# A decoder layer on one core: the column sums of the context's codes move from the matrix engine to accumulating transfers

## The chip, the cores and the metric

The kernel runs on 1 core of one Trainium2 chip. The metric is the device time of one execution in microseconds (us), less is better. The core has a matrix engine (TensorE, "PE" in the profile, with "PEld" for its weight loads), VectorE ("DVE"), ScalarE ("ACT"), GpSimd ("POOL") and a queue of its own for transfers (SyncE, "SP"). Each engine works through its instructions in one order that is fixed when the kernel is built; an instruction that waits holds those behind it on its engine.

## The reference

One decoder layer over `x` (2 x 512 tokens, 1024 wide), cut to what matters:

```python
x = layernorm(x + attention(x))                     # per token, over 32 x 32 head dimensions
# cross step: both operands are rounded to 256 codes, then one product per batch element
def fake_quant(x, s, z):
    q = clip(round(x / s + z), 0, 255)
    return (q - z) * s
x = layernorm(x + fake_quant(x, s1, z1) @ fake_quant(ctx, s2, z2))   # ctx: 2 x 1024 x 1024
...
h = relu(x @ up_w) ** 2
shared = h @ down_w                                  # 1024 -> 2048 -> 1024
moe = ((x @ fc1_w) @ expert_w) * (sum of the two largest of x @ gate_w)
x = layernorm(x + layernorm(shared + moe @ fc2_w) * gamma + beta)
```

The kernel keeps codes, not the dequantised values: `cq` holds 255 minus the code of the context, in two bytes, and `a` holds the code of `x` less 128. Expanding the product of (code - zero point) leaves three terms: the product of the codes, a term per token (`r`), and a term per column that holds the sum of a context's codes over its 1024 rows. That last term is the row `crow`.

## The kernel before, in words

Tokens are worked in 8 tiles of 128 (`t` = 0 to 7), two tiles to a block, four blocks; tiles 0 to 3 belong to context 0, tiles 4 to 7 to context 1. A context is 8 tiles of 128 rows (`KC` = 8), all kept in `cq`.

*The front.* `fill` (L398) projects tiles 2 to 7 to q, k and v, writes them to scratch with accumulating transfers (L195, L196), brings them back later (L179, L180), and makes `e2`, a product of two weights (L458). Beside it `context_tiles` (L537) loads context 0 on SyncE's queue and turns each tile into codes with three ScalarE steps (L375, L378, L381), from 32.6 to 71.5 us.

*The token path* (`token_path`, L683) runs, tile by tile, the scores and attention on VectorE (L474 to L518), a layernorm, then `cross`. Layernorms that run aside (`normalise_aside`) take ScalarE's square and variance (L351, L353), one power on GpSimd (`rstd`, L355), and ScalarE's shift and scaling (L359, L360). `cross` (L616) makes the codes `a` on ScalarE (the last step L644; tile 1 is "hurried" and uses VectorE, L364 to L366), turns them with TensorE (`pta`, L652; L630 for tile 1), copies them out (`aT`), adds `r` and `crow` to the tokens on VectorE (L658, L659), multiplies codes with codes (`py`, L665, two halves of 8 products), and adds the result (L670). The tokens are then turned (`pt_x`, L134) for the feed-forward part.

*The row.* `context_row` (L584) makes `crow` before `cross` of the first tile of a context: two halves, for each a bank `pc` of PSUM, eight products of a matrix of ones with the eight tiles of codes (L591), and one ScalarE step (L594).

*The feed-forward part* of blocks 0 and 1 (`ffn`, products `pu` and `pl` at L827, `pd` at L1057) runs on TensorE beside the token path of the following blocks; blocks 2 and 3 are done together at the end (L942, L1317). `context_beside` (L549) makes the codes of context 1 beside block 0: it loads on GpSimd's queue (L558), does two steps for three tiles early, waits until tile 3's `py` is done (`cq` has one buffer), and writes the rest (L577) from 254.0 to 283.5 us.

*What sets the order.* Instructions are ordered on each engine when the kernel is built, by the order in which the generators above are advanced (the numbers they yield are weights), and by `issue_after`, which lays an instruction behind another one of the same engine. `behind_products` lays the token path's products behind the last feed-forward product laid so far; the `e2` products of the second half are laid behind `codes_turned`, the transposes of tile 1's codes. `spare_bank` (L605) gives a bank of `ps_dn` in the front and while a block's `up` products run, else one of `ps_mm`.

Of the kernel before, what the change touches and what calls it, by code (L numbers as in the profile page):

```python
# [8 lines left out]

F32 = mybir.dt.float32  # L10
BF16 = mybir.dt.bfloat16
AF = mybir.ActivationFunctionType
ALU = mybir.AluOpType
AX = mybir.AxisListType
# [2 lines left out]
P = 128  # L17
# [10 lines left out]
def kernel(  # L28
# [24 lines left out]
    nc = tc.nc  # L53

    B, S, E = x.shape
# [9 lines left out]
    KC = NCTX // P  # L65
# [6 lines left out]
    HALF = 512  # L72
# [30 lines left out]

    ident = const.tile([P, P], F32, name="ident")
    make_identity(nc, ident)
    identb = const.tile([P, P], BF16, name="identb")
    nc.vector.tensor_copy(identb, ident)
    onesb = const.tile([P, P], BF16, name="onesb")
    nc.vector.memset(onesb, 1.0)
    neg_half = const.tile([P, 1], F32, name="neg_half")  # L110
    nc.vector.memset(neg_half, -0.5)

# [115 lines left out]
    def keep_awake(n):  # L228

        ps = ps_mm.tile([P, HALF], F32, tag="mm", name="awake")  # L230
        for _ in range(n):
            laid[0] = nc.tensor.matmul(
                ps.rearrange("p (a b) -> p a b", b=P), onesb,
                onesb.unsqueeze(1).to_broadcast([P, HALF // P, P]), start=True, stop=True,
            )

    qkv = {}
# [100 lines left out]
    def normalise_aside(t, sums, name):  # L338

        n = sums.shape[-1]  # L340
        parts = small.tile([P, 2], F32, tag="parts", name=f"parts_{name}")
        minus = parts[:, 0:1]
        if n > 1:
            minus = small.tile([P, 1], F32, tag="minus", name=f"minus_{name}")
        with behind_acted(True):
            nc.scalar.activation(
                parts[:, 0:n], sums, AF.Copy, scale=-1.0 / E, accum_out=minus if n > 1 else None
            )
        square = attp.tile([P, E], BF16, tag="square", name=f"square_{name}")
        total = small.tile([P, 1], F32, tag="square", name=f"squares_{name}")  # L350
        nc.scalar.activation(square, t, AF.Square, bias=minus, accum_out=total)  # L351
        ve = small.tile([P, 1], F32, tag="ve", name=f"ve_{name}")
        nc.scalar.activation(ve, total, AF.Identity, scale=1.0 / E, bias=eps)  # L353
        rstd = small.tile([P, 1], F32, tag="rstd", name=f"rstd_{name}")
        nc.gpsimd.tensor_tensor(rstd, ve, neg_half, ALU.pow)  # L355
# [176 lines left out]

    made = []

    def context_tiles(b):  # L537

        cq = cqs[b] = tokp.tile([P, KC, E], BF16, tag="cq", name=f"cq_{b}")
        for k in range(KC):  # L540
            stage = work.tile([P, E], F32, tag="work", name=f"ctx_{b}_{k}")
            nc.sync.dma_start(stage, ctx_in[b, ts(k, P), :])
            with tc.issue_after(turned[0].ins):
                for _ in below_top(cq[:, k, :], stage, stage, rs2, z2):
                    pass
            made.append((b, k))
            yield

    def context_beside(b):  # L549
# [17 lines left out]
                yield  # L567
        while b * (S // P) - 1 not in crossed:
            yield
        cq = cqs[b] = tokp.tile([P, KC, E], BF16, tag="cq", name=f"cq_{b}")  # L570
        for k in range(KC):
            if k not in passes:
                passes[k] = below_top(None, stages[k], stages[k], rs2, z2)
            for _ in passes[k]:
                yield
            with behind_acted(True):
                nc.scalar.activation(  # L577
                    cq[:, k, :], stages[k], AF.Relu, scale=-1.0, bias=top_down
                )
            made.append((b, k))  # L580
            load(k + 3)
            yield

    def context_row(b, cq):  # L584
        crow = tokp.tile([P, E], F32, tag="crow", name=f"crow_{b}")
        for h in range(E // HALF):
            pc = spare_bank(f"pc_{b}_{h}")

            with tc.issue_after(projecting[0].ins) if b == 0 else behind_products():
                for k in range(KC):  # L590
                    nc.tensor.matmul(  # L591
                        pc, onesb, cq[:, k, ts(h, HALF)], start=(k == 0), stop=(k == KC - 1)
                    )
# [19 lines left out]

        return tc.issue_after(lately[0].ins) if lately[0] is not None else ExitStack()

    def cross(t, xc, cq, crow, between):  # L616


        hurried = t == TB - 1
        tmp = work.tile([P, E], F32, tag="work", name=f"qt_{t}")  # L620
        a = attp.tile([P, E], BF16, tag="a", name=f"a_{t}")
        aT = tokp.tile([P, KC, P], BF16, tag="aT", name=f"aT_{t}")
        if hurried:

            quantise(a, xc, tmp, rs1, z1)
            yield 2.2
            pt = ps_tr.tile([P, KC, P], BF16, tag="tr", name=f"pta_{t}")
            with behind_products():
                for k in range(KC):
                    codes_turned[0] = nc.tensor.transpose(pt[:, k, :], a[:, ts(k, P)], identb)  # L630
            nc.scalar.copy(aT, pt)
            yield 1.0
            total = ps_tr.tile([P, 2], F32, tag="tr", name=f"pr_{t}")
            with tc.issue_after(expert[0].ins):
                for k in range(KC):
                    nc.tensor.matmul(
                        total, aT[:, k, :], onesb[:, 0:2], start=(k == 0), stop=(k == KC - 1)
                    )
            total = total[:, 0:1]
        else:  # L640
# [5 lines left out]
            )  # L646
            yield 2.0
            yield from between
            pt = ps_tr.tile([P, KC, P], BF16, tag="tr", name=f"pta_{t}")
            with behind_products():  # L650
                for k in range(KC):
                    nc.tensor.transpose(pt[:, k, :], a[:, ts(k, P)], identb)  # L652
            nc.scalar.copy(aT, pt)  # L653
            yield 4.0
        behind = ExitStack if hurried or t == NT - 1 else lambda: tc.issue_after(lowered[0].ins)
        r = small.tile([P, 1], F32, tag="r", name=f"r_{t}")
        with behind():
# [25 lines left out]
    def token_path():  # L683
# [25 lines left out]
        for blk in range(NBLK):  # L709
            xcs = []  # L710
            x2T = []
            for i in range(TB):
# [9 lines left out]
                if t % (S // P) == 0:  # L722
                    b = t // (S // P)
                    while len(made) < (b + 1) * KC:
                        yield 1.0
                    batch = cqs[b], context_row(b, cqs[b])
                between = scores_left(t + 1) if t + 1 < NT else ()
                last = yield from cross(t, xc, *batch, between)

                def hand_over(blk=blk, t=t, i=i, xc=xc, x2T=x2T):  # L730
                    if not x2T:
# [416 lines left out]
    def down_pair(outer):  # L1148
# [118 lines left out]
        def end_aside(i):  # L1267
# [8 lines left out]
            square = attp.tile([P, E], BF16, tag="square", name=f"summed_{i}")  # L1276
# [210 lines left out]
```

## Time and profile before

| | us |
|---|---|
| median of 3 runs (704.29 to 704.39) | 704.35 |
| the profiled execution, its time | 704.49 |
| its span, first to last instruction | 702.7 |
| TensorE busy / VectorE / ScalarE / GpSimd | 682.4 / 586.5 / 261.8 / 77.0 |
| moved by DMA | 139.08 MB, 198 GB/s over the span |
| mean granted TensorE clock | 0.991 |

How to read the views shown later. In an order of time, a row has its start, its length, the engine, the line of the kernel, the operation, the tile written and those read, the sizes and the count, and in brackets the idle time before it and what ended that. In a tile's answer, three lengths in ns are the least, the median and the largest. A DMA row ends with the median time from issue to landing. Products are pipelined, so the length of one is not what it costs TensorE.

### The profile page before, as it was taken

The page shows a single profiled execution, that of the slowest core. Times are in us where ns is not written, and L with a number is a line of the kernel's source. Part 1 is how long each engine was busy: PE and PEld are TensorE (multiplying, and loading weights), DVE is VectorE, ACT ScalarE, POOL GpSimd, SP SyncE. Part 2 cuts the span into 40 slices and gives each one's busy share as a digit, 9 for nine tenths or more (in the row PEclk, how much of TensorE's full clock was granted, in tenths as well). Part 3 has the DMA queues.
Part 4 walks back from the last instruction along what each step waited for, and adds up shares of the span by engine and source line. Part 5 has one row for each costly group of instructions (what it writes and reads, how often), then busy time and mean ns, then how long its engine had stood idle before and what let it go on. Part 6 is the DMA issues. An engine that isn't in the chain of part 4 may idle for free.

```text
span 702.7 us, 7462 instructions
## 1 busy us (share of the span) xinstructions
PE 682.4 (97%) x2812; PEld 482.6 (69%) x2812; DVE 586.5 (83%) x678; ACT 261.8 (37%) x440; POOL 77.0 (11%) x107
## 2 busy tenths in 40 slices
PE   8999999999999999999999999999999999999991
PEld 4666654578876444478876444488888888888881
DVE  5899987699999999799999950397787688897895
ACT  1287544222635458426736132212251200000252
POOL 1012112100011122001002000020010000001012
PEclk9999999999999999999999999999999999999996
DMA  9999528485446458446436534667897445556733
GB/s 336 304 346 370 127 32 290 116 288 175 135 132 174 178 194 254 134 166 215 145 119 177 182 120 126 238 194 242 338 344 254 164 166 171 168 197 192 207 84 120
DMA packets 70900, 139.08 MB, mean 198 GB/s; under 512 B 5264, under 2 KB 39696, under 8 KB 70864
## 3 DMA queue, kind: packets, MB, share of 16 engines
q1 hardware_dynamic: 60656, 106.87, 44.9%
q0 software_dynamic: 10064, 31.47, 16.3%
q8 instruction: 22, 0.36, 0.2%
q10 hardware_dynamic: 144, 0.26, 0.1%
q14 instruction: 14, 0.11, 0.0%
HBM read 114.99 MB, written 21.50 MB: 194 GB/s over the span
## 4 chain that ended last, share of the span: by engine, by line
PE 44%; issue 5%; ACT 3%; DVE 2%; POOL 1%; POOLq 0%
PE pd L1057 9%; PE pp L942 9%; PE ps L1317 7%; PE pp_mm L942 5%; PE pp_tr L942 4%; PE ps_mm L1317 4%; PE ps_tr L1317 3%; PE pu L827 2%; ACT square L351 1%; PE py L665 1%; POOL rstd L355 1%; DVE pav L507 1%; PE pl L827 1%; PE pt_x L134 0%; ACT xc L360 0%
## 5 line engine op out<-in xcount | busy, mean ns | idle before, releaser
L1057 PE MATMUL pd<-dn,h 128*128 128x512 f32 x320 | 139.3, 593 | 0.0
L827 PE MATMUL pu<-x2T,up 128*128 128x256 f32 x512 | 113.1, 380 | 0.8 <-ACT relu L843 0.8
L1057 PEld LDWEIGHTS pd<-dn,h 128*128 128x128 f32 x320 | 60.3, 190 | 71.8 <-issue 71.3
L827 PEld LDWEIGHTS pu<-x2T,up 128*128 128x128 f32 x512 | 96.4, 190 | 15.0 <-ACT relu L843 1.2
L507 DVE TENSOR_TENSOR pav<-s,v 128x2048 f32<-128x2048 f32 x32 | 72.5, 2282 | 0.0
L474 DVE TENSOR_TENSOR pqk<-qk 128x2048 f32<-128x2048 f32 x32 | 72.5, 2283 | 0.0
L480 DVE TENSOR_REDUCE s<-pqk 128x256 f32<-128x2048 f32 x32 | 72.3, 2278 | 0.1
L513 DVE TENSOR_REDUCE o<-pav 128x64 f32<-128x2048 f32 x32 | 72.0, 2266 | 0.0
L157 PE MATMUL pqk<-wqkv,xT 128*128 128x512 f32 x128 | 63.4, 595 | 1.2 <-DVE wqkv L249 0.9
L162 PEld LDWEIGHTS pv<-wqkv,xT 128*128 128x128 f32 x128 | 24.3, 190 | 24.2 <-issue 22.5
L355 POOL TENSOR_TENSOR rstd<-ve,neg_half 128x1 f32<-128x1 f32 x21 | 21.6, 1028 | 174.7 <-ACT ve L353 171.4
L162 PE MATMUL pv<-wqkv,xT 128*128 128x256 f32 x128 | 35.6, 379 | 0.0
L670 DVE SCALAR_TENSOR_TENSOR xc<-py,ns,xc 128x512 f32<-128x512 f32 x16 | 11.7, 743 | 26.4 <-PE py L665 26.4
L157 PEld LDWEIGHTS pqk<-wqkv,xT 128*128 128x128 f32 x128 | 23.6, 190 | 11.4 <-issue 4.3
L843 ACT ACTIVATE relu<-pu 128x256 f32<-128x256 f32 x32 | 12.1, 377 | 51.5 <-PE pu L827 51.5
L665 PE MATMUL py<-cq,aT 128*128 128x512 bf16 x128 | 28.9, 379 | 0.9 <-ACT aT L653 0.9
L1221 DVE TENSOR_TENSOR tt<-dn 128x1024 f32<-128x1024 f32 (+1 forms) x20 | 21.2, 1060 | 10.2 <-DMA dn<-in_L_ffn_down_w_dram 5.8
L458 PE MATMUL pe<-fc,exT 128*128 128x512 f32 x64 | 28.7, 594 | 0.0
L827 PE MATMUL pl<-x2T,fc 128*128 128x256 f32 x128 | 28.2, 380 | 0.5 <-ACT latent L856 0.5
L827 PEld LDWEIGHTS pl<-x2T,fc 128*128 128x128 f32 x128 | 24.2, 190 | 4.3 <-ACT latent L856 0.9
L665 PEld LDWEIGHTS <-aT 128*128 128x128 bf16 x128 | 12.4, 98 | 17.0 <-issue 2.0
L653 ACT COPY aT<-pta 128x1024 bf16<-128x1024 bf16 x7 | 7.0, 1007 | 43.9 <-PE pta L652 43.9
(311 smaller groups left out, 1165.5 us busy)
## 6 DMA issues: line engine op xcount, KB each, us to landing
up<-in_L_ffn_up_w_dram SPq DMA_DIRECT2D x16, 1024.0 KB, 5.5
dn<-in_L_ffn_down_w_dram SPq DMA_DIRECT2D x16, 1024.0 KB, 5.0
pair<-in_L_ffn_up_w_dram SPq DMA_DIRECT2D x8, 1024.0 KB, 6.3
dn<-tw SPq DMA_DIRECT2D x8, 1024.0 KB, 5.1
tw<-outer POOLq DMA_DIRECT2D x7, 1024.0 KB, 5.1
fc<-in_L_ffn_fc_w_dram SPq DMA_DIRECT2D x6, 1024.0 KB, 5.6
dn<-in_L_ffn_down_w_dram SPq DMA_DIRECT2D x12, 512.0 KB, 5.6
outer<-in_L_ffn_down_w_dram SPq DMA_DIRECT2D x5, 1024.0 KB, 5.1
```

The source lines that it names most:

```text
L157: projecting[0] = nc.tensor.matmul(pqk, xT[:, k, :], wqkv[k][:, 0 : 2 * DG], start=(k == 0), stop=(k == KE - 1))
L162: nc.tensor.matmul(pv[:, :DG], xT[:, k, :], wqkv[k][:, 2 * DG : 3 * DG], start=(k == 0), stop=(k == KE - 1),)
L458: expert[0] = nc.tensor.matmul(ps, exT[m // 2][:, m % 2, ts(l, P)], fc2[m // 2][:, m % 2, ts(n, HALF)], start=(m == 0), stop=(m == NL - 1),)
L474: nc.vector.tensor_tensor(prod.rearrange("p (d e g) -> p d e g", d=DC, g=G), q3[:, ts(c, DC), :].unsqueeze(2).to_broadcast([P, DC, D, G]), ...
L480: nc.vector.tensor_reduce(s[:, ts(c, DC), :].rearrange("p d e -> p (d e)"), prod.rearrange("p (c g) -> p c g", g=G), AX.X, ALU.add,)
L507: nc.vector.tensor_tensor(prod.rearrange("p (d g e) -> p d g e", d=DC, g=G), s[:, ts(c, DC), :].unsqueeze(2).to_broadcast([P, DC, G, D]), ...
L513: nc.vector.tensor_reduce(o[:, ts(c, DC), :].rearrange("p d g -> p (d g)"), prod.rearrange("p (c e) -> p c e", e=D), AX.X, ALU.add,)
L665: crossed[t] = nc.tensor.matmul(py, aT[:, k, :], cq[:, k, ts(h, HALF)], start=(k == 0), stop=(k == KC - 1))
L827: lately[0] = nc.tensor.matmul(ps[:, :NB], ws[:, k, wcols], xT[:, k, :], start=(k == 0), stop=(k == KE - 1))
L942: lately[0] = nc.tensor.matmul(banks[m], steps[g][m][:, k, :], moving[m][:, k, :], start=(k == 0 and m not in (6, 3, 7)), stop=(k == KH - ...
L1057: lately[0] = nc.tensor.matmul(pd[i][n], h[:, kk // 4, i, kk % 4, :], w[:, k, ts(n, HALF)], start=(kk == 0), stop=(kk == NK - 1),)
L1317: lately[0] = nc.tensor.matmul(banks[mm], unit(o, mm, j), inner_weights[o, cc][mm][:, j - lo, :], start=(j == 0 and mm not in FIRST_OF), s ...
```

## The change

After each tile of codes is made, a transfer on GpSimd's queue takes it into one more tile in SBUF, `codes_b` (128 x 1024): the first copies, the seven that follow add. Each of the eight accesses the same tile, so each waits for the one before. A sum of eight codes is at most 2040, which a 16-bit float of eleven significant bits holds exactly; `bfloat16` has eight, so all two-byte tiles of the kernel become `float16`. `context_row` then needs one product with the ones for each half instead of eight, and is called later: inside `cross`, after the codes of the context's first token tile are turned, just before `r`, `crow` and `py`.

```diff
-BF16 = mybir.dt.bfloat16
+F16 = mybir.dt.float16
...
-    identb = const.tile([P, P], BF16, name="identb")
+    identh = const.tile([P, P], F16, name="identh")
-    onesb = const.tile([P, P], BF16, name="onesb")
+    onesh = const.tile([P, P], F16, name="onesh")
...
-    made = []
+    made, code_sums = [], {}
+
+    def add_codes(b, k):
+
+        if k == 0:
+            code_sums[b] = tokp.tile([P, E], F16, tag="codes", name=f"codes_{b}")
+            nc.gpsimd.dma_start(code_sums[b], cqs[b][:, k, :])
+        else:
+            nc.gpsimd.dma_start(code_sums[b], cqs[b][:, k, :], accum_op=ALU.add)
 
     def context_tiles(b):
 
-        cq = cqs[b] = tokp.tile([P, KC, E], BF16, tag="cq", name=f"cq_{b}")
+        cq = cqs[b] = tokp.tile([P, KC, E], F16, tag="cq", name=f"cq_{b}")
         for k in range(KC):
             stage = work.tile([P, E], F32, tag="work", name=f"ctx_{b}_{k}")
             nc.sync.dma_start(stage, ctx_in[b, ts(k, P), :])
             with tc.issue_after(turned[0].ins):
                 for _ in below_top(cq[:, k, :], stage, stage, rs2, z2):
                     pass
+            add_codes(b, k)
             made.append((b, k))
             yield
...
                 nc.scalar.activation(
                     cq[:, k, :], stages[k], AF.Relu, scale=-1.0, bias=top_down
                 )
+            add_codes(b, k)
             made.append((b, k))
             load(k + 3)
             yield
 
-    def context_row(b, cq):
+    crows = {}
+
+    def context_row(b):
         crow = tokp.tile([P, E], F32, tag="crow", name=f"crow_{b}")
         for h in range(E // HALF):
             pc = spare_bank(f"pc_{b}_{h}")
 
             with tc.issue_after(projecting[0].ins) if b == 0 else behind_products():
-                for k in range(KC):
-                    nc.tensor.matmul(
-                        pc, onesb, cq[:, k, ts(h, HALF)], start=(k == 0), stop=(k == KC - 1)
-                    )
+                nc.tensor.matmul(
+                    pc, onesh, code_sums[b][:, ts(h, HALF)], start=True, stop=True
+                )
...
-    def cross(t, xc, cq, crow, between):
+    def cross(t, xc, b, between):
 
 
         hurried = t == TB - 1
+        cq = cqs[b]
...
             nc.scalar.copy(aT, pt)
             yield 4.0
+        if b not in crows:
+            crows[b] = context_row(b)
+        crow = crows[b]
         behind = ExitStack if hurried or t == NT - 1 else lambda: tc.issue_after(lowered[0].ins)
...
-                    batch = cqs[b], context_row(b, cqs[b])
+                    batch = b
                 between = scores_left(t + 1) if t + 1 < NT else ()
-                last = yield from cross(t, xc, *batch, between)
+                last = yield from cross(t, xc, batch, between)
```

The other edits rename `BF16`, `identb` and `onesb` to `F16`, `identh` and `onesh` where they are used.

More of the change, by code (lines that the diff above doesn't have):

```diff
@@ L105 @@
     make_identity(nc, ident)
-    identb = const.tile([P, P], BF16, name="identb")
-    nc.vector.tensor_copy(identb, ident)
-    onesb = const.tile([P, P], BF16, name="onesb")
-    nc.vector.memset(onesb, 1.0)
+    identh = const.tile([P, P], F16, name="identh")
+    nc.vector.tensor_copy(identh, ident)
+    onesh = const.tile([P, P], F16, name="onesh")
+    nc.vector.memset(onesh, 1.0)
     neg_half = const.tile([P, 1], F32, name="neg_half")
@@ L232, in keep_awake @@
             laid[0] = nc.tensor.matmul(
-                ps.rearrange("p (a b) -> p a b", b=P), onesb,
-                onesb.unsqueeze(1).to_broadcast([P, HALF // P, P]), start=True, stop=True,
+                ps.rearrange("p (a b) -> p a b", b=P), onesh,
+                onesh.unsqueeze(1).to_broadcast([P, HALF // P, P]), start=True, stop=True,
             )
@@ L348, in normalise_aside @@
             )
-        square = attp.tile([P, E], BF16, tag="square", name=f"square_{name}")
+        square = attp.tile([P, E], F16, tag="square", name=f"square_{name}")
         total = small.tile([P, 1], F32, tag="square", name=f"squares_{name}")
@@ L569, in context_beside @@
             yield
-        cq = cqs[b] = tokp.tile([P, KC, E], BF16, tag="cq", name=f"cq_{b}")
+        cq = cqs[b] = tokp.tile([P, KC, E], F16, tag="cq", name=f"cq_{b}")
         for k in range(KC):
@@ L614, in behind_products @@
         return tc.issue_after(lately[0].ins) if lately[0] is not None else ExitStack()
-    def cross(t, xc, cq, crow, between):
+    def cross(t, xc, b, between):
         hurried = t == TB - 1
+        cq = cqs[b]
         tmp = work.tile([P, E], F32, tag="work", name=f"qt_{t}")
-        a = attp.tile([P, E], BF16, tag="a", name=f"a_{t}")
-        aT = tokp.tile([P, KC, P], BF16, tag="aT", name=f"aT_{t}")
+        a = attp.tile([P, E], F16, tag="a", name=f"a_{t}")
+        aT = tokp.tile([P, KC, P], F16, tag="aT", name=f"aT_{t}")
         if hurried:
@@ L626, in cross @@
             yield 2.2
-            pt = ps_tr.tile([P, KC, P], BF16, tag="tr", name=f"pta_{t}")
+            pt = ps_tr.tile([P, KC, P], F16, tag="tr", name=f"pta_{t}")
             with behind_products():
                 for k in range(KC):
-                    codes_turned[0] = nc.tensor.transpose(pt[:, k, :], a[:, ts(k, P)], identb)
+                    codes_turned[0] = nc.tensor.transpose(pt[:, k, :], a[:, ts(k, P)], identh)
             nc.scalar.copy(aT, pt)
@@ L636, in cross @@
                     nc.tensor.matmul(
-                        total, aT[:, k, :], onesb[:, 0:2], start=(k == 0), stop=(k == KC - 1)
+                        total, aT[:, k, :], onesh[:, 0:2], start=(k == 0), stop=(k == KC - 1)
                     )
@@ L648, in cross @@
             yield from between
-            pt = ps_tr.tile([P, KC, P], BF16, tag="tr", name=f"pta_{t}")
+            pt = ps_tr.tile([P, KC, P], F16, tag="tr", name=f"pta_{t}")
             with behind_products():
                 for k in range(KC):
-                    nc.tensor.transpose(pt[:, k, :], a[:, ts(k, P)], identb)
+                    nc.tensor.transpose(pt[:, k, :], a[:, ts(k, P)], identh)
             nc.scalar.copy(aT, pt)
             yield 4.0
+        if b not in crows:
+            crows[b] = context_row(b)
+        crow = crows[b]
         behind = ExitStack if hurried or t == NT - 1 else lambda: tc.issue_after(lowered[0].ins)
@@ L1275, in end_aside @@
             sums = small.tile([P, 1], F32, tag="sum3", name=f"sum3_{PAIR}_{i}")
-            square = attp.tile([P, E], BF16, tag="square", name=f"summed_{i}")
+            square = attp.tile([P, E], F16, tag="square", name=f"summed_{i}")
             acted[0] = nc.scalar.activation(square, y, AF.Copy, accum_out=sums)
```

## The prediction

> **What bounds the kernel now.** I read the page first, then the two tiles that the change touches (`pc`, `cq`), the chain of waits, TensorE's order of time, the windows, and last GpSimd's order of time with the DMA landings by window.
>
> The page says that TensorE is the fullest engine:
>
> ```profile
> PE 682.4 (97%) x2812; PEld 482.6 (69%) x2812; DVE 586.5 (83%) x678; ACT 261.8 (37%) x440; POOL 77.0 (11%) x107
> ```
>
> The tile `pc` holds the products that the change cuts:
>
> ```profile
> L591 PE MATMUL pc<-cq,onesb x32: 379/379/379, 88.3 to 288.8; 128*128 128x512 bf16 x32
> ```
>
> 379 ns is one product's latency. What it costs TensorE is read from the chain of waits, where sixteen products of the same shape take 3.45 us, 0.216 us each (a group of 16 `pc` starts at 285.57, the next product at 289.02: 3.45 us too):
>
> ```profile
> 411.64 3.45 PE py L665 x16
> ```
>
> TensorE in order of time shows where it meets a wait:
>
> ```profile
> 107.82 0.61 PE L652 MATMUL pta<-identb,a 128*128 128x128 bf16 x8
> 111.75 3.62 PE L665 MATMUL py<-cq,aT 128*128 128x512 bf16 x16
> 122.49 0.62 PE L630 MATMUL pta<-identb,a 128*128 128x128 bf16 x8 [0.25 <-DVE a L366]
> ...
> 264.10 1.04 PE L134 MATMUL pt_x<-ident,xc 128*128 128x128 f32 x8
> 285.57 3.62 PE L591 MATMUL pc<-cq,onesb 128*128 128x512 bf16 x16
> ...
> 323.19 22.07 PE L827 MATMUL pu<-x2T,up 128*128 128x256 f32 x101 [0.82 <-ACT relu L843]
> ...
> 373.05 3.72 PE L827 MATMUL pl<-x2T,fc 128*128 128x256 f32 x16 [0.52 <-ACT latent L856]
> ```
>
> Work is laid in one fixed order, so work taken out ahead of a wait is handed back at that wait. At 122.49 TensorE already waits for token tile 1's codes, which VectorE sets. The remaining e2 products cannot be brought in front of it: the code lays them behind `codes_turned`.
>
> GpSimd's order of time shows the queue into which the new transfers go, and VectorE's shows who is behind it:
>
> ```profile
> 79.53 0.87 POOL L195 DMA_DIRECT2D qkv_d<-qk  x1 [9.69 <-ACT qk L189]
> 80.64 1.44 POOL L355 TENSOR_TENSOR rstd<-ve,neg_half 128x1 f32<-128x1 f32 x1
> ```
>
> ```profile
> 89.45 0.16 DVE L658 TENSOR_TENSOR r<-total,s12d 128x1 f32<-128x1 f32 x1 [2.96 <-ACT a L644]
> ```
>
> The rstd of token tile 0 (80.64) feeds ScalarE's normalisation and codes `a`, and VectorE stands 2.96 us for them. A delay of that rstd is a delay of VectorE, and VectorE sets the 122.49.
>
> Landing times of an accumulating transfer of 256 KB (`qkv_d<-qk`), asked by window (36 to 50, 50 to 62, 62 to 75, 75 to 90 us):
>
> ```profile
> qkv_d<-qk POOLq DMA_DIRECT2D x1, 256.0 KB, 5.1
> ...
> qkv_d<-qk POOLq DMA_DIRECT2D x1, 256.0 KB, 6.8
> ...
> qkv_d<-qk POOLq DMA_DIRECT2D x1, 256.0 KB, 7.3
> ...
> qkv_d<-qk POOLq DMA_DIRECT2D x1, 256.0 KB, 4.2
> ```
>
> **Part by part.** The sum is made against the profiled execution: span 702.7, its time 704.49 us, 0.14 above the median 704.35; I subtract from the median at the end.
>
> *Products.* Each context keeps 2 of 16: 14 x 0.216 = 3.02 us less TensorE per context, 6.05 in all. ScalarE's two `crow` steps (0.78 each) stay.
>
> *Context 0 gains nothing on TensorE.* Its 16 products run at 88.3. TensorE would reach 122.49 three microseconds earlier and wait there for `a` of tile 1. Only VectorE's chain counts. On it, the 0.79 us that VectorE waits for `py` of tile 0 (at 115.4) goes, because `py` comes 3 us earlier: -0.8.
>
> *Context 1 gains 3.02.* After 285.57 the token codes are ready long before TensorE turns them: tile 4's end at 286.9 and are turned at 304.0, tile 5's at 346.9 and 354.6, tile 6's at 388.8 and 409.3, tile 7's at 426.7 and 444.1. The waits at 323.19 and 373.05 are for ScalarE steps queued behind the normalisations of tiles 4 and 5, which themselves follow `py`, so they should move along with TensorE; VectorE's 2.2 us steps make that inexact: +0.2, bounds 0 and 3.0 (all lost).
>
> *Sixteen transfers on GpSimd's queue.* No row has a transfer of 16-bit floats from SBUF into SBUF; the nearest are the 256 KB rows above, 4.2 quiet and 5.1 to 7.3 loaded, and 256 KB fetched in 3.0. I take the accumulating rows, by their window. Each add waits on GpSimd for the one before, and whatever is queued behind waits too: the stores of `qkv_d`, fetches of `qk`, `v`, the loads of context 1, ln_beta, and rstd. Context 0: codes 0 end at 38.1; then 5.1 + 5.1 + 6.8 + 6.8 + 7.3 + 7.3 + 4.2 = 42.6, so the eighth add issues at 80.7, takes 0.86 on GpSimd, and rstd starts at 81.6 instead of 80.64: +0.9. Bounds: 0 (landings of 3 us, or rstd ahead in the queue) and +9.4 (all at 7.3). The stores behind them have five buffers; `qk` of tile 2, fetched at 50.4, is wanted at 66.9.
>
> The Trainium skill (DMA: Bandwidth & Descriptors, "Anatomy of one DMA") puts a transfer from this queue at about 2.0 us plus bytes over 436 GB/s, an estimate of 2.6 us for 256 KB, where this trace shows 4.2 to 7.3; by the page the chain would keep up with the codes and the +0.9 would be 0. The same page ("Two DMAs through the same engine are not ordered") has the dependent transfer wait for the semaphore of the first, which speaks against eight in a row; no run here shows them yet.
>
> The DMA engines are full there (share 0.98 to 1.05 from 40 to 70). `qkv_d`'s 0.29 MB took 13.0% of 14 us, so eight adds take some 13 us of all 16 engines. The cover is slack: TensorE's next `xs` is issued 10 us or more before it is turned, and ScalarE waits only 1.0 us for `ctx`. Without it, the codes and with them the adds slip.
>
> Context 1: codes end at 255.1, 256.2, 257.4. The first transfer (a copy; 256 KB fetches land in 3.0) would land by 258.8; the second waits for it, and rstd of tile 3, at 259.03, starts about 1.0 later. ScalarE has 0.5 of slack before it, and TensorE's `pt_x` at 264.10 has 0.2 (xc ends at 263.89). I take +0.5, bounds 0 and 4.7 (a further add of 4.2 in front). Later rstds (275.55) have the slack of tile 4's codes, 17 us less 3. Codes 7 end at 283.5, so the sums land by 288.
>
> *The row is moved* to just before `py` (111.75 and 307.95). Behind the new wait on TensorE stand all later products, but the sums land by 86 and 288: 0. VectorE's L659 (1.28 us) moves from 96.14 and 293.76 to behind `crow`: same total; tile 0's `crow` should be ready near 110.6, when VectorE comes by (o ends 110.7): 0, bounds -0.3 and +2.2 (one VectorE step). For context 1 the row now takes `ps_dn` banks: four are wanted at 305, and block 0's last is read until 305.92: +0.3, bounds 0 and 1.0.
>
> *16-bit floats.* No row has float16. Two-byte products cost 0.216, four-byte ones 0.43 (`pd`, 4 in 1.72); ScalarE writes bf16 in 1.14 and f32 in 1.23, VectorE in 0.69 either way. I take 0 by width; the far bound is 128 x 0.216 = 27.6 us (`py` at the four-byte price), the near one 0: no row is quicker.
>
> Sum: -3.02 + 0.2 - 0.8 + 0.9 + 0.5 + 0.3 = -1.9; 704.49 becomes 702.6, the median 702.4.
>
> **Rivals.**
>
> *B, slower: the eighth add holds rstd at 80.64.* Place: GpSimd's queue. The sum allows 0.9; slower begins when rstd starts 2.8 late, at 83.4, so the eighth add at 82.6: a mean landing of (82.6 - 38.1) / 7 = 6.4 us. At 6.8 (the row of 50 to 62) it issues at 85.7, rstd starts at 86.6, 5.9 late: -1.9 - 0.9 + 5.9 = +3.1, 707.5. For it: DMA engines full, and the adds themselves load them. Against: from 75 us on they are at 0.4 to 0.6, landing in 4.2; the scratch rows go to DRAM, the adds stay in SBUF. 0.33.
>
> *C, no change: context 1's 3.0 us go at 323 and 373.* Neither relu nor latent moves earlier, because VectorE keeps tiles 4 and 5 where they are: -1.9 - 0.2 + 3.0 = +0.9, 705.3; with the adds out of rstd's way 704.4. For it: VectorE is full from 140 to 400. Against: the slack of the codes above. 0.20.
>
> *D, both contexts pay:* -6.05, 698.3. It needs tile 1's codes 3 us earlier, and VectorE is busy 94% or more of every stretch of 10 us from 30 to 80. 0.02.
>
> *E, the change doesn't do what it says:* TensorE reaches `pc` before the sums. Context 0's would have to land after 108, a mean of (108 - 38.1) / 8 = 8.7 us each. +3 or more. 0.04.
>
> **How the numbers follow.** The forecast (A) has 0.41, near 702.4, from 700.9 (no term against it but the banks) to 702.9. A change of 0.2% (1.4 us) is about what a measurement of this kernel can tell from none. Faster: A and D, 0.43. Same: C, 0.20. Slower: B and E, 0.37. The range 700.9 to 707.8 takes in A, C and two thirds of B.
>
> **What would show it.** `pc` x4 just ahead of `py`; TensorE waiting about 3 us for L366 ahead of `pta` of tile 1; `pt_x` of tile 3 near 264.5; group `pu` of block 1 2 to 3 us earlier; rstd near 81.6. Adds that land in over 6.4 us before rstd, or a wait of TensorE for `crow`, `codes` or `aT` over 1 us, would prove it wrong; so would `py` slower than 0.216 each.

## The result and the profile after

The changed kernel takes 722.11 us (median of 4 runs, 721.25 to 722.88) where the kernel before, on the same chip, takes 704.37: a ratio of 1.0237, 95% interval 1.0221 to 1.0254, so 17 us slower. The profiled execution took 721.86 us with a span of 720.1 (before 704.49 and 702.7). Line numbers from here on are those of the kernel shown.

TensorE's work is less by the 28 products, and yet its busy time is not:

```profile
PE 683.6 (95%) x2784; PEld 482.5 (67%) x2784; DVE 586.3 (81%) x678; ACT 261.1 (36%) x440; POOL 89.0 (12%) x123
```

The products are gone as announced: the tile `pc` has 4, and none of them waits for a sum of codes, only for its bank (the reader of a bank is `y`):

```profile
L602 PE MATMUL pc<-codes,onesh x4: 376/378/379, 108.8 to 317.6; 128*128 128x512 f16 x4
...
  DVE y L1021: 0.8, 2
```

So the time has to be in waits. TensorE in order of time shows two places:

```profile
94.91 2.07 PE L157 MATMUL pqk<-wqkv,xT 128*128 128x512 f32 x2 [6.38 <-ACT xT L135]
...
128.68 0.62 PE L642 MATMUL pta<-identh,a 128*128 128x128 f16 x8 [0.31 <-DVE a L366]
...
269.70 1.09 PE L134 MATMUL pt_x<-ident,xc 128*128 128x128 f32 x8 [0.98 <-ACT xc L360]
...
307.00 5.41 PE L842 MATMUL pu<-x2T,up 128*128 128x256 f32 x16 [2.38 <-ACT lg L799]
...
316.92 0.38 PE L602 MATMUL pc<-codes,onesh 128*128 128x512 f16 x1 [0.55 <-DVE y L1021]
...
321.77 5.30 PE L680 MATMUL py<-cq,aT 128*128 128x512 f16 x16 [3.81 <-DVE y L1021]
...
344.38 24.44 PE L842 MATMUL pu<-x2T,up 128*128 128x256 f32 x112 [2.57 <-ACT relu L858]
...
372.33 0.61 PE L664 MATMUL pta<-identh,a 128*128 128x128 f16 x8
```

In the kernel before, the turn of tile 5's codes stands at

```profile
354.60 0.61 PE L652 MATMUL pta<-identb,a 128*128 128x128 bf16 x8
```

Tile 1's codes are turned at 128.68 (before 122.49: 6.2 later). Tile 5's are turned at 372.33 (before 354.60: 17.7 later). The end is 17.4 later. So 6.2 us are lost in the front, 11.5 between 128 and 372, and none after. From `pt_x` to tile 5's turn TensorE idles 9.8 us, where it idled 0.8 before.

**The front.** GpSimd in order of time; `L541` is the copy, `L543` the adds, `L195` and `L196` the stores that were there before:

```profile
38.40 0.57 POOL L541 DMA_DIRECT2D codes<-cq  x1 [28.93 <-ACT cq L381]
44.60 0.90 POOL L543 DMA_DIRECT2D codes<-cq  x1 [5.63 <-DMA codes<-cq]
...
85.91 0.86 POOL L543 DMA_DIRECT2D codes<-cq  x1 [3.00 <-issue]
...
87.58 1.58 POOL L355 TENSOR_TENSOR rstd<-ve,neg_half 128x1 f32<-128x1 f32 x1
```

Each add waits for the landing of the one before (where the bracket says `issue`, the profile shows no releaser). From the copy to the eighth transfer pass 85.91 - 38.40 = 47.5 us, 6.8 for each of seven links. Taken one at a time, the seven land 5.6, 6.0, 8.2, 7.6, 7.3, 5.5 and 3.3 us after their start, 43.5 together; the other 4.0 us are the 0.5 to 0.6 us that pass, in every link, between a landing and the start of the next add. Two stores stand behind the eighth transfer, and the rstd of token tile 0 stands behind them: 87.58 instead of 80.64. ScalarE's next row, and then VectorE's:

```profile
89.19 0.29 ACT L359 ACTIVATE shift<-rstd,parts 128x1 f32<-128x1 f32 x1 [8.95 <-POOL rstd L355]
```

```profile
96.52 0.16 DVE L673 TENSOR_TENSOR r<-total,s12d 128x1 f32<-128x1 f32 x1 [9.62 <-ACT a L656]
```

VectorE waits 9.62 us for the codes `a`, 2.96 before: 6.7 more, of which 6.2 arrive at TensorE's turn of tile 1. TensorE's 6.38 us at 94.91 come from the same rstd: the copies `xT` stand behind it on ScalarE (94.30 instead of 87.23). They are not what sets the turn of tile 1, which still waits for VectorE.

**Context 1.** GpSimd again, later; `L567` loads a tile of the context:

```profile
281.93 0.88 POOL L567 DMA_DIRECT2D ctx<-in_ctx_dram  x1
287.65 0.85 POOL L543 DMA_DIRECT2D codes<-cq  x1 [4.84 <-issue]
288.20 0.87 POOL L567 DMA_DIRECT2D ctx<-in_ctx_dram  x1
295.16 0.85 POOL L543 DMA_DIRECT2D codes<-cq  x1 [6.09 <-issue]
295.73 0.87 POOL L355 TENSOR_TENSOR rstd<-ve,neg_half 128x1 f32<-128x1 f32 x1
```

Each load now stands behind an add, and each add behind a landing: the last two loads go out at 281.93 and 288.20 (before 263.05 and 271.07), and the rstd of tile 4 at 295.73 (before 275.55). ScalarE works in order and stands for a load, and far behind it comes a step that has nothing to do with the codes, the exponential of tile 5's scores:

```profile
288.39 1.24 ACT L375 ACTIVATE ctx<-ctx,z,rs 128x1024 f32<-128x1024 f32 x1 [10.24 <-DMA ctx<-in_ctx_dram]
...
304.52 1.04 ACT L493 ACTIVATE s<-s 128x1024 f32<-128x1024 f32 x1
```

VectorE waits for that exponential:

```profile
305.60 1.22 DVE L499 TENSOR_REDUCE den<-s 128x32 f32<-128x1024 f32 x1 [15.20 <-ACT s L493]
```

In the kernel before, VectorE already waited at this place, for the codes `a` of tile 4 and then for the exponential:

```profile
287.07 0.16 DVE L658 TENSOR_TENSOR r<-total,s12d 128x1 f32<-128x1 f32 x1 [2.85 <-ACT a L644]
288.01 1.22 DVE L499 TENSOR_REDUCE den<-s 128x32 f32<-128x1024 f32 x1 [0.79 <-ACT s L493]
```

Behind it on VectorE is the output of block 0 (`y`), the last reader of the banks that `pc` and `py` need, and so TensorE's 0.55, 0.28 and 3.81; and behind that the tokens' `xc`, whose normalisation delays the relu (2.57). The 2.38 for `lg` is ScalarE's lateness too: that copy stands at 306.60, behind the exponential and the codes `a` (before, at 297.12). There is a second price. In the windows (stretch, its length, busy time with number of instructions of PE, PEld, DVE, ACT, POOL, the granted clock, DMA share, GB/s) the clock falls after TensorE's waits:

```profile
90.00:100.00 10.00, 5.09 (x8) 2.72 (x9) 2.69 (x3) 8.31 (x11) 1.74 (x2) 0.67 0.29 59
...
310.00:315.00 5.00, 5.00 (x26) 4.18 (x25) 5.00 (x5) 1.70 (x3) 0.00 (x0) 0.81 0.10 18
...
320.00:325.00 5.00, 3.23 (x9) 1.22 (x9) 5.00 (x7) 0.00 (x0) 0.54 (x1) 0.71 0.61 216
```

Over the rows themselves, 307.0 to 312.2 and 321.8 to 326.9, it is 0.67. That fits the sixteen products of `py` at 321.77, which take 5.30 us and not 3.62, and the sixteen `pu` at 307.00, which take 5.41 and not 3.72.

### The profile page after: what moved, and what is told of

Read it like the earlier page. It is cut to its first block, busy times and chain, and to the rows that moved or that the text cites. A ratio compares the mean times of both kernels' runs of the same rounds, so it can differ in the third digit from the quotient of the medians.

```text
span 720.1 us, 7440 instructions
## 1 busy us (share of the span) xinstructions
PE 683.6 (95%) x2784; PEld 482.5 (67%) x2784; DVE 586.3 (81%) x678; ACT 261.1 (36%) x440; POOL 89.0 (12%) x123
## 3 DMA queue, kind: packets, MB, share of 16 engines
q1 hardware_dynamic: 60656, 106.87, 43.5%
## 4 chain that ended last, share of the span: by engine, by line
PE 45%; DVE 4%; ACT 3%; issue 1%; POOL 1%; DMA 1%; POOLq 0%; DVEq 0%; ACTq 0%
PE pd L1072 9%; PE pp L957 8%; PE ps L1332 6%; PE pp_mm L957 5%; PE pu L842 4%; PE pp_tr L957 4%; PE ps_mm L1332 2%; PE pl L842 2%; PE ps_tr L1332 2%; PE py L680 1%; ACT square L351 1%; DMA y_a<-xc 1%; POOL rstd L355 1%; ACT y_a L360 0%; DVE tt L1236 0%
## 5 line engine op out<-in xcount | busy, mean ns | idle before, releaser
L842 PE MATMUL pu<-x2T,up 128*128 128x256 f32 x512 | 115.3, 385 | 5.2 <-ACT relu L858 2.8
L157 PE MATMUL pqk<-wqkv,xT 128*128 128x512 f32 x128 | 65.3, 610 | 7.7 <-ACT xT L135 6.7
L680 PE MATMUL py<-cq,aT 128*128 128x512 f16 x128 | 30.6, 395 | 4.7 <-DVE y L1021 3.8
L680 PEld LDWEIGHTS <-aT 128*128 128x128 f16 x128 | 12.8, 101 | 22.7 <-issue 8.8
L499 DVE TENSOR_REDUCE den<-s 128x32 f32<-128x1024 f32 x8 | 9.7, 1217 | 20.8 <-ACT s L493 20.8
```

Of the source, the lines that this page charges most:

```text
L157: projecting[0] = nc.tensor.matmul(pqk, xT[:, k, :], wqkv[k][:, 0 : 2 * DG], start=(k == 0), stop=(k == KE - 1))
L680: crossed[t] = nc.tensor.matmul(py, aT[:, k, :], cq[:, k, ts(h, HALF)], start=(k == 0), stop=(k == KC - 1))
L842: lately[0] = nc.tensor.matmul(ps[:, :NB], ws[:, k, wcols], xT[:, k, :], start=(k == 0), stop=(k == KE - 1))
```

## The experiments

Theory: the adds are dear as *waits on GpSimd's queue*, for what stands behind them (rstd, loads). Rivals: float16 is slow; the transfers load the DMA engines; the moved row costs the time; the banks do. In most runs the builder lays a new order on VectorE and ScalarE, because it plans with the changed work; where two runs are compared closely, I say how far their orders agree. The time is the median of several executions; the rows are those of one of them, up to 4.6 us off that median. Differences in us are the ratio times 704.4.

**float16 alone** (kernel before):

```diff
-BF16 = mybir.dt.bfloat16
+BF16 = mybir.dt.float16
```

> The kernel before with its two-byte tiles in float16 instead of bfloat16; products, places and transfers as before. Theory (the whole 17.7 us come from the transfers' place on GpSimd's queue): 704.4 within 0.5, and a group of 16 py products costs 3.45 us as before. Rival (float16 itself costs on some engine): above 705.5, with py above 0.216 us each or the ScalarE steps that write codes above 1.14 us.

Measured 1.0011 (1.0000 to 1.0022), +0.8 us, at most 1.5 and a little over what was expected; `py` keeps 0.216 us for each product. float16 is not the cause of the 17 us. In the profiled execution TensorE waits 2.07 us for a relu at 324.00 (0.82 before), although VectorE's order from 280 to 326 is that of the kernel before: tile 4's `a` came 0.8 later. A wait of 1 or 2 us at this relu alone is therefore no sure sign of an edit.

**The change without sums** (no transfer; the row from the first tile's codes only):

```diff
-            add_codes(b, k)
...
-                    pc, onesh, code_sums[b][:, ts(h, HALF)], start=True, stop=True
+                    pc, onesh, cqs[b][:, 0, ts(h, HALF)], start=True, stop=True
```

> The changed kernel without any of its sixteen transfers: the row is made from the first tile of codes alone, so seven of eight tiles are left out of the column sums; the place of the row and its four products are those of the change. This is the most that the cut of products can bring. Theory (context 0's 3.0 us are handed back at the turn of tile 1's codes, context 1's are kept): 700.5 to 702.5. Rival 1 (moving the row costs in itself, by banks of PSUM that block 0 still holds): 704.5 or more, with TensorE waiting for the last reads of block 0's output ahead of pc or py. Rival 2 (both contexts pay): 698.3.

Measured 0.9971 (0.9952 to 0.9989), -2.0 us. This is what 28 removed products are worth here if the sums are free. TensorE in order of time shows context 0's share handed back:

```profile
121.70 1.04 PE L640 MATMUL pta<-identh,a 128*128 128x128 f16 x8 [2.53 <-DVE a L366]
```

The turn comes 0.8 us earlier, not 3. Part of context 1's share goes too: waits for relu of 1.37, 0.78 and 0.48 us at 321 to 330, 2.6 against 0.82 before. The execution of these rows took 706.23 us, 3.4 over the median: it is 0.6 us ahead of the kernel before when tile 7's codes are turned (443.52 against 444.12) and loses 2.4 after that, behind the part that was changed.

**One context at a time** (the other by sixteen products, at the changed place):

```diff
     def add_codes(b, k):
+        if b not in (0,):      # the second run: (1,)
+            return
...
+                for k in range(1 if b in (0,) else KC):
```

> Transfers for context 0 alone; context 1's row by sixteen products from its codes, at the place of the change. Theory (rstd of tile 0 is held on GpSimd behind the eighth transfer, which costs 6.2 us at the turn of tile 1's codes): 710.0 to 711.5, rstd near 87.6, the turn near 128.7. Rival (the delay of the front comes from the transfers of both contexts or is made up later): below 708.

> Transfers for context 1 alone; context 0's row by sixteen products from its codes, at the place of the change. Theory (the loads of context 1's last tiles stand on GpSimd behind transfers that wait for each other and for codes, which makes the codes, the rstd of tile 4 and VectorE late): 714 to 716.5, ScalarE waiting about 10 us for a load of ctx. Rival (context 1 is late only because the front came late, or the two delays share one cause): 701 to 706.

Measured 1.0103 (1.0086 to 1.0120), +7.3 us, and 1.0138 (1.0123 to 1.0153), +9.7 us. The sum, 17.0, agrees with the change's 16.7 (each of the two also holds the moved row and float16, +1.3 by a run below, so the sum counts these twice; the intervals are over 1 us wide to either side). With transfers for context 0 alone tile 1 is turned at 128.82; for context 1 alone at 122.14, and `py` of tile 4 waits 3.82 us for `y` as in the change. These are two losses, each there without the other.

**The front: two chains of four for context 0** (odd and even tiles, four products with ones; context 1 by products):

```diff
-        if k == 0:
-            code_sums[b] = tokp.tile([P, E], F16, tag="codes", name=f"codes_{b}")
+        if k < 2:
+            code_sums[b, k] = tokp.tile([P, E], F16, tag=f"codes{k}", name=f"codes_{b}_{k}")
...
-            nc.gpsimd.dma_start(code_sums[b], cqs[b][:, k, :], accum_op=ALU.add)
+            nc.gpsimd.dma_start(code_sums[b, k % 2], cqs[b][:, k, :], accum_op=ALU.add)
```

> Transfers for context 0 alone, in two chains (even and odd tiles) into two tiles, and two products for each half; context 1's row by sixteen products. Each transfer waits for the one before the last. Theory (rstd is held by the length of the one chain): the eighth transfer issues by 76 to 78 and rstd starts near 80.6 to 81.5, 0 to 1.5 us above the kernel before where one chain cost 7.4. Rival (full DMA engines make the transfers land late however they are chained): rstd at 84 or later, 3.5 us above or more.

Measured 1.0046 (1.0029 to 1.0063), +3.2 us. GpSimd and TensorE in order of time:

```profile
77.63 0.86 POOL L545 DMA_DIRECT2D codes<-cq  x1 [1.02 <-ACT cq L381]
...
81.55 1.24 POOL L355 TENSOR_TENSOR rstd<-ve,neg_half 128x1 f32<-128x1 f32 x1
```

```profile
122.52 0.62 PE L647 MATMUL pta<-identh,a 128*128 128x128 f16 x8 [2.19 <-DVE a L366]
```

The same eight transfers, but the eighth issues at 77.63 (one chain: 85.91), rstd starts at 81.55 (87.58) and tile 1 is turned at 122.52 (128.68, and 122.49 before). A single transfer lands no sooner: 8.8 us in the median, with two in flight. So it is the waiting in line, not the traffic, that cost the front its 6.2 us. The time is above the 0 to 1.5 us expected all the same. The front is not where it is lost: TensorE waits 0.84 and 2.19 us for relu at 319 to 326, as in the next run, which itself costs 1.3; the other 1.9 are not accounted for.

**The moved row alone** (no transfer, sixteen products at the changed place):

```diff
     def add_codes(b, k):
+        if b not in ():
+            return
```

> The change without any transfer: sixteen products per context in 16-bit floats, at the changed place of the row (behind the turning of the first token tile's codes). It is the baseline of the runs that keep sixteen products at the new place. Theory (the 2 to 4 us that these runs still lose have to do with transfers beside the context's codes): the move alone costs 0 to +1 us, and no wait of over 1 us on TensorE at 300 to 325. Rival (the new place costs them): +2 to +4 us, the waits for relu at 318 to 327 already there without a transfer.

Measured 1.0018 (1.0003 to 1.0034), +1.3 us: neither quite free nor the 2 to 4 of the rival. VectorE's `xc + r + crow` (L679) now stands behind block 0's output and two `pav`, so `xc` after `py` ends at 317.64 instead of 314.98, and TensorE waits 0.96 and 2.19 us for relu (0.82 before). But this kernel is in float16 too, and float16 at the old place measured +0.8, turned tile 5's codes as late (357.07; here 356.97) and had such a wait. A price of the move itself is not shown beyond the 0.5 us between the two, which lies within their intervals.

**The traffic alone** (sixteen products at the changed place, and each tile of codes also sent, unchained, to a scratch tensor in DRAM):

```diff
-            nc.gpsimd.dma_start(code_sums[b], cqs[b][:, k, :], accum_op=ALU.add)
+        nc.gpsimd.dma_start(code_sums[b][k], cqs[b][:, k, :])
```

> Both rows by sixteen products at the place of the change, and beside them all sixteen transfers of 256 KB on GpSimd's queue in the places of the change, each into a piece of scratch of its own in DRAM, so that none waits for another; nothing reads them. Theory (the waits of the chain, not the traffic or the issues, cost the time): 0 to 2 us above the kernel before, rstd of tile 0 within 1.5 us of 80.6, ScalarE waiting less than 3 us for any load of ctx. Rival (traffic, descriptor writing and queue places cost it even without a chain): 6 us above or more.

Measured 1.0057 (1.0040 to 1.0074), +4.0 us, over what I expected. The front is clean (tile 1 turned at 122.41). In context 1 the loads land in a median of 8.5 us instead of 4.8, ScalarE stands 5.54 for one, and rstd of tile 4 starts at 282.40 instead of 275.55. Less the 1.3 of the moved row, about 2.7 us are traffic and its issue. These transfers write to DRAM and do not add, so they are a stand-in for the adds' traffic, not the same.

**Context 1's loads on other queues** (transfers for context 1 only, one chain). Loads of tiles 3 to 7 from ScalarE's queue:

```diff
-                nc.gpsimd.dma_start(stages[k], ctx_in[b, ts(k, P), :])
+                (nc.gpsimd if k < 3 else nc.scalar).dma_start(stages[k], ctx_in[b, ts(k, P), :])
```

> Transfers for context 1 alone, as in the run with transfers for context 1 alone, but the loads of context 1's tiles 3 to 7 are issued from ScalarE's queue instead of GpSimd's, so none stands behind a transfer. Theory (the 9 us of context 1 are the loads behind the chain): ScalarE waits under 3 us for any load, the row's banks are free in time, and the time is 3 us below to 1 us above the kernel before. Rival (the rstd of tiles 3 and 4 behind the chain, not the loads, is the cost): 5 us above or more with rstd of tile 4 still 8 us late.

Measured 1.0027 (1.0009 to 1.0045), +1.9 us instead of +9.7, a little over the theory's bound. With all loads on SyncE's queue instead:

```diff
-                nc.gpsimd.dma_start(stages[k], ctx_in[b, ts(k, P), :])
+                nc.sync.dma_start(stages[k], ctx_in[b, ts(k, P), :])
```

> As the run before it, but all eight loads of context 1 are issued from SyncE's queue, where they stand among the loads of block 0's weights. Theory: as there, 3 us below to 1 us above the kernel before, unless the loads stand behind weights that wait for a buffer; then ScalarE waits for ctx again, and the time is 2 to 6 us above. Rival (rstd behind the chain): 5 us above or more with no wait for ctx.

Measured 1.0169 (1.0106 to 1.0232), +11.9 us, with four executions from 712.77 to 723.02. That is the rival's forecast. ScalarE's waits for `ctx` are down to 0.53 us, yet rstd of tile 4 starts at 289.01, the exponential comes at 298.10 (286.94 before) and `py` waits 3.8 for `y`. So an early landing is not what saved the first of the two, which has rstd as late (288.02). They differ in the order that the builder laid on VectorE: with ScalarE's queue, block 0's output stands ahead of tile 5's first `pav` and its last bank is read from 305.1; with SyncE's it stands behind and it is read from 312.3. So what stands behind the late step matters. The rows do not settle the whole difference: the two profiled executions, 710.50 and 712.77, are 2.3 us apart, the medians 10.1.

**Context 1 in two chains**, loads on GpSimd's queue as in the change, context 0 by products:

```diff
+        if b not in (1,):
+            return
...
+            nc.gpsimd.dma_start(code_sums[b, k % 2], cqs[b][:, k, :], accum_op=ALU.add)
```

> As the run with transfers for context 1 alone (+9.7 us), but the eight tiles go into two chains of four (odd and even tiles, four products with ones at the end): an add waits for the transfer before the last one. Theory (the loop load, codes, add, load: each add holds GpSimd's queue for what is left of one landing): held for half as long, rstd of tile 4 comes before 283 (295.7 in the change), codes by 300, and the cost falls to +1 to +5 us. Rival (the transfers themselves, or the banks, cost the time): +8 us or more stays.

Measured 1.0107 (1.0084 to 1.0130), +7.5 us: a miss, between theory and rival. rstd of tile 4 does come at 282.97 (295.73 in the change), and tile 4's codes are done at 294.5, in time for their turn at 300.98. But a load still lands late (ScalarE waits 6.11 for it), and VectorE and TensorE in order of time are:

```profile
293.49 1.22 DVE L499 TENSOR_REDUCE den<-s 128x32 f32<-128x1024 f32 x1 [9.42 <-ACT s L493]
```

```profile
309.66 6.34 PE L685 MATMUL py<-cq,aT 128*128 128x512 f16 x16 [3.70 <-DVE y L1026]
...
330.60 30.39 PE L847 MATMUL pu<-x2T,up 128*128 128x256 f32 x128 [3.80 <-ACT relu L863]
```

The token codes are in time and it does not help: the exponential and, through it, the banks set the time. Here block 0's output (`y`) follows that row at 303.42, 10 us behind, much as in the kernel before (299.67 behind 288.01). In the last run below, with one chain and the loads on ScalarE's queue, it follows 3 us behind (299.23 behind 296.17), and there an exponential later than this one goes with +1.9 only. After either wait the clock is at 0.50 over 5 us (309.66 to 314.66, 330.60 to 335.60), and the sixteen products of `py` take 6.34.

**Sums without a transfer** (context 1 added on GpSimd's own lanes, context 0 by products at the old place):

```diff
-            nc.gpsimd.dma_start(code_sums[b], cqs[b][:, k, :], accum_op=ALU.add)
+            nc.gpsimd.tensor_tensor(
+                out=code_sums[b], in0=cqs[b][:, k, :],
+                in1=code_sums[b] if k > 1 else cqs[b][:, 0, :], op=ALU.add,
+            )
```

> No transfer at all: context 0 by sixteen products at the old place; context 1's eight tiles are added by seven additions on GpSimd's own lanes (128 x 1024 two-byte each), then two products. No row shows such an addition; bounded by VectorE's 0.69 us for two-byte 128 x 1024 steps below, and 4 us above. Theory (what costs is the wait for a landing on GpSimd's queue and the transfers' load, not the place of the addition): each add ends 1 to 4 us after its codes, nothing is held for longer than one add, -2 to +1 us. Rival (the additions slow VectorE's steps beside them, which is full there): VectorE's steps between 255 and 290 get longer than before, +1 to +6 us.

Measured 1.0002 (0.9986 to 1.0017): no difference. An addition takes 2.1 to 3.8 us on GpSimd and waits for no landing. But VectorE in order of time has

```profile
267.14 1.22 DVE L518 TENSOR_TENSOR o<-o,rden 128x256 f32<-128x256 f32 x1
...
273.82 7.68 DVE L474 TENSOR_TENSOR pqk<-qk 128x2048 f32<-128x2048 f32 x2
```

where these take 0.41 and 4.48 in the kernel before: 4.0 us more, beside the additions at 265.93 to 268.07 and 273.10 to 279.35. The time is the theory's; the rival's mechanism is there, but its price of 1 us or more does not arrive.

**Two chains, loads on ScalarE's queue, context 0 by products at the old place:**

```diff
                     batch = b
+                    if b == 0:
+                        crows[b] = context_row(b)
```

> The best version with transfers that the runs point to: context 0 by sixteen products at the old place, context 1 in two chains of four with the loads of tiles 3 to 7 on ScalarE's queue. Theory: the adds hold rstd of tile 4 by under 5 us, and of context 1's 2.6 us of removed products at most what the run without sums kept (2.0) is left: -1.5 to +1 us. Rival (eight more transfers beside the loads cost time whatever they hold, as eight unchained ones did): +1.5 to +4 us.

Measured 700.94 us (700.75 to 701.97) against 704.93 for the kernel before: 0.9939 (0.9915 to 0.9962), -4.3 us. It beats both kernels, and is faster than theory and rival had it. Since that is more than the sums can bring, three runs take it apart: the kernel before with the same loads on ScalarE's queue; the version above with sixteen products in place of sums; and the version above with one chain.

```diff
+                (nc.gpsimd if k < 3 else nc.scalar).dma_start(stages[k], ctx_in[b, ts(k, P), :])   # all three
...
+        if b not in ():             # the second of the three: no transfer
+            return
...
+            nc.gpsimd.dma_start(code_sums[b], cqs[b][:, k, :], accum_op=ALU.add)   # the third: one chain
```

> The kernel before, with the loads of context 1's tiles 3 to 7 on ScalarE's queue and nothing else changed: no 16-bit sums, no float16, sixteen products at the old places. Theory (the gain of the version with two chains is the sums' 2.6 us of removed products and about as much again from the loads, which no longer stand behind GpSimd's work): -1 to -2 us. Rival (all of its 4.0 us are the loads and the order that the builder plans with them): -3 to -4.5 us. Third (all from the sums): within 0.7 us of before.

> As the version with two chains (-4.0 us), but no transfer at all: context 1's row by sixteen products at the changed place; float16, context 0 by products at the old place, loads on ScalarE's queue. Theory: 3.0 us more TensorE work than with two chains, at 305, where that version has no wait of TensorE from 265 to 375: -2 to -0.5 us against before. Rival (the sums bring nothing, the loads all): -3 to -4.5 us.

> As the version with two chains (-4.0 us), but all eight tiles of context 1 in one chain; the order on VectorE and ScalarE is the same but for two places. Theory (a chain holds rstd of tile 4, on ScalarE's order ahead of tile 5's exponentials, and VectorE waits for these): rstd of tile 4 at 286 to 290 (283.1 with two chains), VectorE's wait for the exponentials longer by as much, +3 to +7 us against two chains, so -1 to +3 against before. Rival (context 0's place made the 6 us between the two earlier runs): -3 to -4.5 us against before.

| | ratio to before | us | rstd tile 4 | VectorE's wait for the exponential | tile 5 turned |
|---|---|---|---|---|---|
| before | 1 | 0 | 275.55 | 0.79 | 354.60 |
| loads moved, nothing else | 0.9969 (0.9957 to 0.9980) | -2.2 | 280.71 | 8.04 | 353.56 |
| loads moved, row moved, products | 0.9968 (0.9956 to 0.9980) | -2.3 | 280.12 | none | 353.91 |
| loads moved, two chains | 0.9939 (0.9915 to 0.9962) | -4.3 | 283.06 | 0.69 | 351.09 |
| loads moved, one chain | 1.0027 (1.0016 to 1.0038) | +1.9 | 287.48 | 5.53 | 356.71 |

The column of VectorE's wait is for the exponential alone: before, 2.85 us for `a` stand just ahead of it, and in each of the last three rows, which are in float16, 5.8 us for TensorE's `pd`. About half of the -4.3 is the loads and the order planned with them; the other 2.0 go to the sums, of 12 x 0.216 = 2.6 us of products saved, as far as runs can be compared in which VectorE's order differs in several places. The two last rows have VectorE's order the same but for two places and ScalarE's but for one; between them lies the chain alone, 6.2 us:

```profile
291.62 1.22 DVE L499 TENSOR_REDUCE den<-s 128x32 f32<-128x1024 f32 x1 [0.69 <-ACT s L493]
```

with two chains, and with one

```profile
296.17 1.22 DVE L499 TENSOR_REDUCE den<-s 128x32 f32<-128x1024 f32 x1 [5.53 <-ACT s L493]
```

The rival of that run (context 0's place made the difference) falls: with one chain the old place and the changed place both cost +1.9. With two chains TensorE has no wait at all from 265 to 375. A long wait for the exponential need not hurt, as the second row of the table shows (8.04): there block 0's banks are read by 301.9 (before 305.9), and tile 4's `xc` after `py` is done at 313.5 (before 315.0).

## Why the prediction was wrong

**Right.** Context 0's products bring TensorE nothing: 2.53 and 2.19 us of wait for L366 appear at tile 1's turn, and the turn gained 0.8. float16 costs what bfloat16 does. TensorE never reaches `pc` before the sums (rival E). Rival D did not occur. The ceiling was sized -3.3 by the forecast's terms without the transfers (-3.02 + 0.2 - 0.8 + 0.3) and measured -2.0: at rival C's place, the relu at 321 to 330, the waits of the profiled execution are 1.8 us longer.

**Wrong, first step: "5.1 + 5.1 + 6.8 + 6.8 + 7.3 + 7.3 + 4.2 = 42.6, so the eighth add issues at 80.7", rstd of tile 0 at 81.6.** The mechanism was named, and the landings were sized well: the seven took 43.5 us. What the sum put at nothing is the time between a landing and the start of the next add, 4.0 us in seven links, and the two stores behind the eighth. With 0.3 us at the first transfer the add came at 85.9, 5.2 late, and rstd at 87.58, 6.0 late. The kernel before shows the gap, in the fetch that waits for the store of 44.73; that store landed 5.1 us after its start, at 49.8:

```profile
50.41 0.58 POOL L179 DMA_DIRECT2D qk<-qkv_d  x1 [3.85 <-DMA qkv_d<-qk]
```

Rival B put the eighth add at 85.7, and rstd 5.9 us late; it came 6.9 late and cost 6.2 us. That B was so near is in part luck: it took 6.8 us for a landing, and the landings had a mean of 6.2, below the 6.4 from which B was to decide. It was the link, landing and gap, that took 6.8.

The Trainium skill (DMA: Bandwidth & Descriptors, "Anatomy of one DMA — SWDGE (gpsimd) path") would have a transfer of 256 KB from this queue done in about 2.0 us plus bytes over 436 GB/s, by estimate 2.6 us. The sixteen transfers here (two copies, fourteen adds) landed in 2.3 to 8.2, 5.7 in the median: the formula is near the quickest one only.

**Wrong, second step: "Later rstds (275.55) have the slack of tile 4's codes, 17 us less 3."** This is the larger one: +0.5 was set, bounds to 4.7, and context 1 costs 9.7 by itself, 11.5 in the change. I looked at one follower of that rstd, TensorE's turn of `a`, and it had the slack. Behind the same rstd on ScalarE's order stands the exponential of tile 5's scores, and VectorE had 0.79 us of *wait* for it in the kernel before, right behind 2.85 us for the codes `a` themselves (its step `r`, 287.07), so no slack whatever. And I listed "the loads of context 1" among what waits behind an add and gave them no price. They make a loop: a load waits behind an add, the codes wait for the load, the next add waits for the codes. It moved the last load by 17 us, and ScalarE's wait of 10.24 us for the load before it stands ahead of tile 4's rstd.

**Not settled: "VectorE's L659 moves ... same total", banks +0.3.** Total busy time stayed, its place did not: with the moved row the step stands behind block 0's output, and `xc` after `py` ends 2.7 us later than before, 1.9 later than in float16 alone. The time with the moved row, +1.3, is not told apart from that of float16 alone, +0.8.

**The range.** It was built with one unknown at its bound at a time. B's 5.9 and context 1's 4.7 were never added, though both hang on the same landing time; together they give -1.9 - 0.9 + 5.9 - 0.5 + 4.7 = 7.3, 711.7. Even with the far bounds of both, 9.4 and 4.7, it would be 715.2. The rest, to 722, stood behind a follower that I had not priced.

**Open.** How much of context 1's 11.5 us is load of the DMA engines, and how much waiting, can't be divided exactly: the builder laid another order in each run. The nearest figures are 2.7 for unchained traffic, to DRAM, and 6.2 for one chain against two, with the loads on ScalarE's queue. That the clock follows TensorE's waits was seen, not varied.

## What to carry to other kernels

A chain of dependent transfers costs its issuing queue the whole landing time of each link, and the gap until the next one starts: write down everything that the queue carries between the links (scalar powers, loads, stores), and for each of these *every* follower on the next engine's order, not the one that the change is about. A wait that already exists in the profile, however short (0.79 us), marks a path without slack; what a longer wait there costs depends on what stands behind it (8.04 us cost nothing with block 0's output close behind). With context 1 in two chains, and its later loads off that queue, about 2.0 us of the 2.6 that its removed products had promised were kept.

## What the runs showed of the hardware

- 256 KB from SBUF into SBUF (a copy and five adds) landed in 6.3 us in the median at 255 to 300, where the kernel before fetches 512 KB in 4.8 on the same queue (250 to 310).
- Between the landing of a transfer and the start of the add that waited for it passed 0.5 to 0.6 us, in all seven links of the front's chain.
- Waits of 3.7 to 3.8 us on TensorE were followed by a granted clock of 0.5 to 0.7 over the next 5 us. The Trainium skill (TensorE: Matmul & The Clock Gate, "What's actually happening") has the clock halved after an idle window of about 3.4 us. That agrees with the `py` of the two chains for context 1 (0.50 after 3.70 us). But shorter waits lowered it too: 0.67 after 2.38 us (the change, 307.0 to 312.2), 0.76 after 2.07 (float16 alone, 325 to 330), while 2.19 us left it at 1.00 (the moved row alone). What decides after a wait of 2 us is not shown.
- An addition on GpSimd stretched VectorE's two-tensor steps beside it from 2.24 to 3.84 us each. The Trainium skill (SBUF — State Buffer, "Who interferes with whom") says that a VectorE instruction with two inputs in SBUF contends with a GpSimd instruction that reads SBUF, one blocking the other; 4.0 us over three steps is that price here.
